# Layer 0 of a graph-attention stack: accumulators of half a PSUM bank, fed row by row, and a fourth bank for search products

## The chip, the cores and the metric

The kernel runs on one core of a Trainium2 chip. The metric is the device time of one execution in microseconds (us), as the median of three runs. A separate profiled execution gives the trace that is read here.

## The reference

Four graph-attention layers follow each other on 3327 nodes with 256 features; after each layer the input is added and the rows are normalised. The change is in layer 0 alone:

```python
g_src = nodes @ W_src_w.T + W_src_b
g_tgt = nodes @ W_tgt_w.T + W_tgt_b
g = leaky_relu(g_src[:, None, :] + g_tgt[None, :, :], 0.2)
score = einsum('ijc,c->ij', g, a_w)
score = where(adj_mat != 0, score, -inf)
weights = softmax(score, axis=1)
x = layernorm(nodes + weights @ g_tgt)
```

The adjacency matrix is random with about 1% ones, so a node has some 32 neighbours and at most 56. Layers 1 to 3 work on the same adjacency matrix densely.

## The kernel before

Layer 0 is the function `sparse0`. It works only on existing edges. The nodes form 26 tiles of 128 rows, in four sets of 4, 7, 9 and 6 tiles (`SETS`). Two kinds of work run side by side.

**The search** (`neighbours`, from L523) finds, for each row, the column numbers of its ones. A row of 3327 columns is cut into seven banks (six of 512 columns and one of 255). `convert` (L535, ScalarE) turns a loaded piece of the adjacency matrix to bf16. `fill` (L548, TensorE) makes, per bank, a product in PSUM that holds the column number where there is a one (the buffers `v`). `scan` (L572, VectorE) takes the eight largest of each of five stretches of that bank (L579). After seven banks `sort` and `note` (L581, L594) make the list of the tile. The loop at L644 walks over the banks: at position g it issues the product of bank g+2 and then the scan of bank g. The buffers of tag `v` are three PSUM banks used in turn, and `pss` (L482, the projection of a tile's source rows), `key_row` (L622), `sorted` (L702) and `early` (L1129) take their turn among them. When a set is searched, its rows are put in order of their number of neighbours, so that a tile needs only as many gathers as its longest row (`LEVELS`, `SEATS`).

**The attention** walks through the gather parts (`parts`, L308), each up to four neighbours of one tile. GpSimd fetches one neighbour's row for each of the 128 nodes with one indirect DMA (L912, into buffers `g`), and VectorE scores it (L932 and L938, against `a_ps`, a PSUM bank in which small products of `excess` also lie: L781, L803, L823). When a tile is scored, `weights` makes the softmax weights, and `combine` (L997) adds up the weighted rows: ScalarE scales each row in place (L1012), TensorE adds it to a PSUM accumulator by a product with the identity (L1015). The accumulator `acc` is a full bank of two halves of 256 columns, and two neighbours at a time (512 columns) are added, one into each half. `add_input` (L1035) then scales and adds both halves (L1041 and L1045), and the sum is written out by GpSimd. There are two such accumulator banks; `pt` (L467, the projection of a tile's target rows) uses the same two.

The eight PSUM banks are: accumulators 2, `v` 3, `a_ps` 1, `minus` 2 (the source row of a tile, negated, L925).

The order on every engine is written out by hand: a loop over the parts (L1282) takes some steps of the search (spread so that a set's lists are there in time, `owed`), then the actions that are due at this part (`due`: `combine` in the eight parts after a tile's last one, `add_input` at the tenth, L1237 to L1239), then the gather of the part eight places ahead, then the scoring. The first set is searched ahead of that, together with the projection of all target rows (`targets`, L461), which fill the table that is gathered from (L1178 to L1201). The last tile adds only its first four parts on TensorE and the rest on VectorE (`add_aside`, L982). Layer 1 follows at once (L1723, products with the dense attention weights), and its TensorE work is queued behind that of layer 0.

Of the kernel before, what the change touches and what calls it, by code (L numbers as in the profile page):

```python
# [19 lines left out]
P = 128  # L20
# [30 lines left out]
def gat_stack(  # L51
# [226 lines left out]
    def sparse0(lost):  # L278
        GROUP, TURNS, LEAD, SPREAD = 4, 22, 8, 8
        starts = [sum(SETS[:s]) for s in range(len(SETS))]  # L280
        with ExitStack() as s0:
# [179 lines left out]
            def targets(it):  # L461

                xt, pn = columns_of(it)
                row = io0.tile([P, ROW], F32, tag="row", name="row", bufs=3)
                if pn < P:
                    nc.vector.memset(row, 0.0)
                pt = ps0.tile([P, BANK], F32, tag="acc", name="pt")  # L467
                project(pt, xt, pn, w_tgt)
                yield
                nc.scalar.copy(row[:pn], pt[:pn, :ROW])  # L470
                nc.gpsimd.dma_start(table_d[1 + it * P : 1 + it * P + pn, :], row[:pn])
                if it < SETS[0]:
                    nc.gpsimd.dma_start(own_rows(it)[:, AT_TGT:], row)
                elif pn < P:
                    nc.gpsimd.dma_start(own_rows(it)[pn:, AT_TGT:], row[pn:])
                yield

            def sources(it):

                xt, pn = columns_of(it)  # L480
                yield
                pss = ps0.tile([P, BANK], F32, tag="v", name="pss", bufs=3)  # L482
                project(pss, xt, pn, w_src, bs_row)
                yield
                minus = find.tile([P, dim + 1], F32, tag="minus", name="minus")
                if pn < P:
                    nc.vector.memset(minus, 0.0)
                    nc.scalar.dma_start(own_rows(it)[pn:, AT_X : AT_X + dim], minus[pn:, :dim])
                nc.scalar.mul(minus[:pn], pss[:pn, : dim + 1], -1.0)  # L489
                nc.scalar.dma_start(own_rows(it)[:, : dim + 1], minus)  # L490
                yield
# [26 lines left out]
            listed = {}  # L518

            def steps_of(s):  # L520
                return SETS[s] * (len(banks_n) + 2) + 8

            def neighbours(s):  # L523

# [23 lines left out]
                def fill(t, b):  # L548
                    lo, hi = banks_n[b]
                    w, at0 = hi - lo, lo % PIECE  # L550
                    adj_b = cast[t, lo // PIECE]
                    v = filled[t, b] = ps0.tile([P, BANK], F32, tag="v", name="v", bufs=3)
                    nc.tensor.matmul(v[:, :w], leads[:, b, :], code[:, :w], start=True, stop=False)  # L553
                    own0 = (starts[s] + t) * P
                    own = lo <= own0 < hi
                    nc.tensor.matmul(  # L556
                        v[:, :w], raised, adj_b[:, at0 : at0 + w], start=False, stop=not own
                    )
                    if own:
                        wo = min(P, hi - own0)  # L560
                        nc.tensor.matmul(
                            v[:, own0 - lo : own0 - lo + wo], raised, minus_one[:, :wo],
                            start=False, stop=True,
                        )
                        flag = find.tile([P, P], BF16, tag="flag", name="flag", bufs=1)
                        nc.vector.scalar_tensor_tensor(
                            flag[:, :wo], adj_b[:, own0 % PIECE : own0 % PIECE + wo], 1.0,
                            ident[:, :wo], op0=ALU.mult, op1=ALU.mult,
                            accum_out=marks[:, starts[s] + t, 1:2],
                        )  # L570
# [48 lines left out]
                    return key_diag  # L619

                def spread_key(t, key_diag):
                    row = ps0.tile([P, BANK], F32, tag="v", name="key_row", bufs=3)  # L622
                    nc.tensor.matmul(row[:, :P], ones, key_diag, start=True, stop=True)
                    return row

# [15 lines left out]
                for k in all_pieces[:3] if s else ():  # L641
                    load(s, *k)
                convert(*all_pieces[0])
                for g in range(-2, len(units)):  # L644
                    if g >= 0:
                        t, b = units[g]
                        if b in (1, 2, 3):
                            turn_key(t - 1, b - 1)
                        if b == 0:
                            of_rows[t] = sources(starts[s] + t)  # L650
                        if b in (0, 4, 5):
                            next(of_rows[t])
                    if g + 2 < len(units):
                        t, b = units[g + 2]
                        if b % 2 == 0:
                            at = all_pieces.index((t, b // 2))
                            if at + 1 < len(all_pieces):
                                convert(*all_pieces[at + 1])
                            if at + 3 < len(all_pieces):
                                load(s, *all_pieces[at + 3])  # L660
                        fill(t, b)
                    if g >= 0:
                        t, b = units[g]
                        scan(t, b)
                        if b == len(banks_n) - 1:
                            yield
                            sort(t)
                            yield
                            note(t)
                    yield  # L670
# [17 lines left out]
            def permute(size, ranks, ranks_i, payloads):  # L688
# [10 lines left out]
                )  # L699
                cols = size * (KMAX + 2)  # L700
                assert cols <= BANK and n >= P
                sorted_ps = ps0.tile([P, BANK], F32, tag="v", name="sorted", bufs=3)  # L702
                for t in range(size):
                    unit = io0.tile([P, P], F32, tag="key_diag", name="unit")
                    nc.vector.tensor_scalar(
# [178 lines left out]
            def combine_excess(s):  # L884
                over = extras[s]
                rows = over["g"][:, 0, :dim]
                nc.scalar.activation(rows, rows, AF.Copy, scale=over["weight"][:, 1:2])
                nc.tensor.matmul(
                    held[s, 0]["acc"][:, 0, :], over["back"], rows, start=False, stop=False
                )  # L890

            def gather_own(s, t):
# [85 lines left out]
                )  # L978

            ASIDE = 4  # L980

            def add_aside(entry, k0, k1, first):  # L982

# [13 lines left out]
            def combine(s, t, i):  # L997

                entry = held[s, t]
                kt, w = places[s, t], entry["w"]  # L1000
                cuts = cuts_of(seats[s, t])
                k0, k1 = cuts[i]
                final = seats[s, t]
                if (s, t) == tiles[-1]:
                    final = cuts[ASIDE - 1][1]
                    if i >= ASIDE:
                        add_aside(entry, k0, k1, first=i == ASIDE)
                        return
                g = entry["g"][k0]

                def scale(rows, k):
                    nc.scalar.activation(rows, rows, AF.Copy, scale=w[:, k : k + 1])  # L1012

                def add_up(dst, rows, start=False, stop=False):
                    nc.tensor.matmul(dst, ident, rows, start=start, stop=stop)  # L1015

                if i == 0:
                    entry["acc"] = ps0.tile([P, 2, dim], F32, tag="acc", name="acc0")
                    own_row = entry["own"][:, AT_TGT : AT_TGT + dim]
                    scale(own_row, kt)  # L1020
                for k in range(k0, k1):
                    scale(g[:, k - k0, :dim], k)
                acc, m = entry["acc"], k1 - k0
                pairs = [g[:, k : k + 2, :dim] for k in range(0, m - 1, 2)]
                if i == 0:
                    for x, rows in enumerate(pairs):
                        add_up(acc, rows, start=x == 0)
                    add_up(acc[:, 0, :], own_row)
                else:
                    if m % 2:  # L1030
                        add_up(acc[:, 1, :], g[:, m - 1, :dim])
                    for x, rows in enumerate(pairs):
                        add_up(acc, rows, stop=k1 == final and x == len(pairs) - 1)

            def add_input(s, t):  # L1035

# [2 lines left out]
                nc.vector.reciprocal(inv, entry["total"])  # L1039
                y = entry["y"] = io0.tile([P, dim], F32, tag="hs", name="hs")  # L1040
                nc.vector.scalar_tensor_tensor(  # L1041
                    y, entry["acc"][:, 0, :], inv, entry["own"][:, AT_X : AT_X + dim],
                    op0=ALU.mult, op1=ALU.add,
                )
                nc.vector.scalar_tensor_tensor(  # L1045
                    y, entry["acc"][:, 1, :], inv, y, op0=ALU.mult, op1=ALU.add
                )
                nc.vector.tensor_add(y, y, bt_rows)
                if "aside" in entry:
# [76 lines left out]
                    rows1.append(t)  # L1126

            def early_bank():
                return ps0.tile([P, BANK], F32, tag="v", name="early", bufs=3)  # L1129

            def dots_next(x):
                for c in range(kc):
# [43 lines left out]


            first = neighbours(0)  # L1178
            next(first)
            next(first)  # L1180
            score_columns()
# [982 lines left out]
```

## Time and profile before

| | us |
|---|---|
| median of three runs | 3398.66 (3390.78 to 3407.27) |
| the profiled execution | 2952.55 |
| its span | 2950.7 |
| GpSimd: gathers (L912), 894 of them | 851.6 busy, first start 88.6, last start 1342.6 |
| first layer-1 product on TensorE (L1723) | 1367.12 |

The profiled execution is 446 us shorter than the median of the runs; the profile shows only itself. Layer 0 takes the span's first 1367 us, layers 1 to 3 the rest. In the page's slices, a digit is a busy share in tenths. In the timeline, a line is the start, the duration, the engine, the line of the kernel, what is written from what, and in brackets how long the engine had been idle and what ended that. In the list of waits, a line is who waited for whom, the total, how many times, and the longest.

### The profile page before, as it was taken

The page shows a single profiled execution, that of the slowest core. Times are in us where ns is not written, and L with a number is a line of the kernel's source. Part 1 is how long each engine was busy: PE and PEld are TensorE (multiplying, and loading weights), DVE is VectorE, ACT ScalarE, POOL GpSimd, SP SyncE. Part 2 cuts the span into 40 slices and gives each one's busy share as a digit, 9 for nine tenths or more (in the row PEclk, how much of TensorE's full clock was granted, in tenths as well). Part 3 has the DMA queues.
Part 4 walks back from the last instruction along what each step waited for, and adds up shares of the span by engine and source line. Part 5 has one row for each costly group of instructions (what it writes and reads, how often), then busy time and mean ns, then how long its engine had stood idle before and what let it go on. Part 6 is the DMA issues. An engine that isn't in the chain of part 4 may idle for free.

```text
span 2950.7 us, 45073 instructions
## 1 busy us (share of the span) xinstructions
PE 2317.0 (79%) x15862; PEld 1359.2 (46%) x15862; DVE 2134.7 (72%) x5615; ACT 852.4 (29%) x2381; POOL 992.3 (34%) x1061
## 2 busy tenths in 40 slices
PE   7466667556545416657899999999999999999997
PEld 4222323222222103325688888763546567534332
DVE  6789789968776518755455521138999999999997
ACT  3244445434334304533344411110010110111211
POOL 2676767777777777772000000000000000000000
PEclk8576777777767757889999999999999999999998
DMA  7685655545644435545776733331222222212211
GB/s 234 194 263 147 187 166 171 141 130 158 166 112 114 112 107 124 171 120 165 227 208 195 201 82 107 110 98 45 73 61 84 75 80 63 73 43 62 59 47 48
DMA packets 183854, 370.50 MB, mean 126 GB/s; under 512 B 35772, under 2 KB 124707, under 8 KB 182596
## 3 DMA queue, kind: packets, MB, share of 16 engines
q1 hardware_dynamic: 103994, 178.49, 21.4%
q0 software_dynamic: 51008, 155.70, 19.1%
q10 hardware_dynamic: 28618, 33.33, 3.3%
q8 instruction: 128, 2.10, 0.3%
q14 instruction: 106, 0.87, 0.1%
HBM read 327.52 MB, written 46.23 MB: 127 GB/s over the span
## 4 chain that ended last, share of the span: by engine, by line
PE 46%; DVE 4%; DMA 2%; issue 0%; ACT 0%; SPq 0%; DVEq 0%; POOL 0%; POOLq 0%; ACTq 0%
PE acc L1773 18%; PE acc L1723 16%; PE acc L1781 9%; DVE e L1629 3%; PE misc L1557 3%; DMA at<-at_d 1%; PE misc L1666 0%; DMA at_d<-at 0%; DMA at_i<-in_adj_t_dram 0%; DVE stats L1952 0%; DVE h L1950 0%; DVE h L1745 0%; DVE both L1947 0%; PE misc L1822 0%; DMA dst<-in_l_att_dram 0%
## 5 line engine op out<-in xcount | busy, mean ns | idle before, releaser
L912 POOL DMA_INDIRECT g<-table_d,lst x894 | 851.6, 953 | 273.1 <-issue 245.6
L1629 DVE SCALAR_TENSOR_TENSOR e<-rate,feat,at 128x896 f32<-128x896 f32 (+4 forms) x832 | 843.6, 1080 | 59.2 <-PE acc L1781 47.7
L1015 PE MATMUL acc<-g,ident 128*128 128x512 f32 (+1 forms) x896 | 505.5, 708 | 262.3 <-ACT g L1012 246.1
L1773 PE MATMUL acc<-e,feat 128*32 128x384 f32 (+2 forms) x6656 | 692.7, 515 | 6.7 <-DVE h L1745 4.2
L1773 PEld LDWEIGHTS acc<-e,feat 128*32 128x32 f32 x6656 | 307.1, 110 | 300.2 <-issue 161.5
L1015 PEld LDWEIGHTS acc<-g,ident 128*128 128x128 f32 x896 | 195.1, 228 | 481.6 <-ACT g L1012 364.6
L1781 PE MATMUL acc<-e,feat 128*32 128x384 f32 (+3 forms) x3328 | 383.3, 512 | 0.0
L1012 ACT ACTIVATE g<-g,w 128x256 f32<-128x256 f32 x883 | 365.4, 495 | 0.4 <-ACT minus L489 0.4
L932 DVE TENSOR_TENSOR y<-g,minus_ps 128x1028 f32<-128x1028 f32 (+2 forms) x233 | 273.4, 1173 | 125.0 <-DMA g<-table_d,lst 115.9
L938 DVE SCALAR_TENSOR_TENSOR y<-y,a_ps 128x257 f32<-128x257 f32 x894 | 324.3, 418 | 24.8 <-PE a_ps L781 6.2
L1723 PE MATMUL acc<-feat,e 128*128 128x257 f32 (+2 forms) x1352 | 303.5, 382 | 9.1 <-DVE inv L1744 6.4
L1723 PEld LDWEIGHTS acc<-feat,e 128*128 128x128 f32 (+2 forms) x1352 | 254.9, 191 | 46.9 <-issue 9.3
L1723 PE MATMUL acc<-feat,at 128*128 128x257 bf16 (+2 forms) x2028 | 237.9, 274 | 4.2 <-DMA at<-at_d 4.0
L1781 PEld LDWEIGHTS acc<-e,feat 128*32 128x32 f32 (+1 forms) x3328 | 162.0, 110 | 130.8 <-issue 88.1
L1723 PEld LDWEIGHTS <-at 128*128 128x128 bf16 (+2 forms) x2028 | 198.8, 99 | 38.0 <-DMA at<-at_d 4.5
L553 PE MATMUL v<-code,leads 65*128 65x512 bf16 (+1 forms) x182 | 83.1, 458 | 156.9 <-DVE cand L579 111.0
L1629 DVE SCALAR_TENSOR_TENSOR e<-rate,feat,at_i 128x896 f32<-128x896 f32 (+2 forms) x104 | 112.3, 1081 | 92.1 <-DMA at_i<-in_adj_t_dram 44.6
L579 DVE MAX8 cand<-v 128x8 f32<-128x104 f32 (+2 forms) x858 | 158.9, 260 | 21.7 <-PE v L556 21.7
L1609 POOL DMA_DIRECT2D rate3b_d<-rate_rows x4 | 2.1, 520 | 449.8 <-ACT rate_rows L1608 449.8
L251 POOL TENSOR_TENSOR rstds<-rstds,minus_half 128x7 f32<-128x7 f32 (+1 forms) x8 | 12.0, 1506 | 385.0 <-DVE rstds L250 385.0
L1959 POOL TENSOR_TENSOR rstds<-rstds,minus_half 128x7 f32<-128x7 f32 (+1 forms) x4 | 7.6, 1912 | 384.5 <-DVE rstds L1958 384.5
L1656 ACT CAST at<-at_i 128x896 bf16<-128x896 int32 (+2 forms) x104 | 92.1, 885 | 111.9 <-DMA at_i<-in_adj_t_dram 75.5
(253 smaller groups left out, 1864.6 us busy)
## 6 DMA issues: line engine op xcount, KB each, us to landing
adj_i<-in_adj_dram SPq DMA_DIRECT2D x75, 512.0 KB
at<-at_d SPq DMA_DIRECT2D x150, 224.0 KB
at_i<-in_adj_t_dram SPq DMA_DIRECT2D x50, 448.0 KB
at<-at_d SPq DMA_DIRECT2D x75, 192.0 KB
at<-at_d SPq DMA_DIRECT2D x75, 191.8 KB
g<-table_d,lst POOLq DMA_INDIRECT x894, 2.8
at_d<-at ACTq DMA_DIRECT2D x50, 224.0 KB
at_i<-in_adj_t_dram SPq DMA_DIRECT2D x25, 384.0 KB
```

Source lines behind the costliest of these rows:

```text
L579: nc.vector.max(spread[:, c0 + c, :], view(v[:, :w]))
L912: nc.gpsimd.indirect_dma_start(out=g[:, k - k0, :], out_offset=None, in_=table_d[:, :], in_offset=bass.IndirectOffsetOnAxis(ap=entry["lst" ...
L932: nc.vector.tensor_tensor(y, rows, minus_src[:, None, :].to_broadcast([P, m, dim + 1]), op=ALU.max)
L938: nc.vector.scalar_tensor_tensor(y, y, 1.0, a_ps[:, : dim + 1], op0=ALU.mult, op1=ALU.mult, accum_out=sc)
L1012: nc.scalar.activation(rows, rows, AF.Copy, scale=w[:, k : k + 1])
L1015: nc.tensor.matmul(dst, ident, rows, start=start, stop=stop)
L1557: nc.tensor.matmul(pacc[:pn, : dim + self.extra], ht[:, k, :pn], self.weight[:, k, :], start=(k == 0), stop=(k == kc - 1),)
L1629: nc.vector.scalar_tensor_tensor(e[:pn, : c1 - c0], self.rate[b][:pn, h_of, : c1 - c0], q, at[:pn, : c1 - c0], op0=ALU.max, op1=ALU.mult,)
L1656: nc.scalar.copy(at[:pn, :w], at_i[:pn, :w])
L1723: nc.tensor.matmul(accs[s][:pn, : dim + 1], a[:pj, s * P : s * P + pn], f[:pj, : dim + 1], start=(j == 0 and part == 0), stop=(j == nt - 1 ...
L1773: nc.tensor.matmul(accs[x][p][q : q + 32, : hi - lo], f[:pj, at0 : at0 + 32], es[at0 // hd][:pj, lo:hi], start=(j == 0), stop=(j == nt - 1),)
L1781: nc.tensor.matmul(accs[x][pairs][h_of * 32 : (h_of + 1) * 32, : hi - lo], f[:pj, dim + h_of : dim + h_of + 1].to_broadcast([pj, 32]), es[ ...
```

## The change

It has two parts, both in layer 0.

An accumulator is now half a bank. One bank (`both`, tag `acc`, one buffer) is allocated once, and the tiles use its two halves in turn. `combine` adds each scaled row by itself, 256 columns wide, the tile's own row first. `add_input` has one operation less, since there is one sum instead of two.

The bank that this frees goes to the tag `v`, which now has four. The search issues the product of bank g+3, instead of g+2, ahead of the scan of bank g; the loop has one step more at its beginning, which the plan (`steps_of`) and the first calls take into account. The projection `pt` moves from the two banks of tag `acc` to the two of tag `minus`.

```diff
-                pt = ps0.tile([P, BANK], F32, tag="acc", name="pt")
+                pt = ps0.tile([P, BANK], F32, tag="minus", name="pt")
...
-                pss = ps0.tile([P, BANK], F32, tag="v", name="pss", bufs=3)
+                pss = ps0.tile([P, BANK], F32, tag="v", name="pss", bufs=4)
...
-                return SETS[s] * (len(banks_n) + 2) + 8
+                return SETS[s] * (len(banks_n) + 2) + 9
...
-                    v = filled[t, b] = ps0.tile([P, BANK], F32, tag="v", name="v", bufs=3)
+                    v = filled[t, b] = ps0.tile([P, BANK], F32, tag="v", name="v", bufs=4)
...
-                for g in range(-2, len(units)):
+                for g in range(-3, len(units)):
...
-                    if g + 2 < len(units):
-                        t, b = units[g + 2]
+                    if g + 3 < len(units):
+                        t, b = units[g + 3]
...
-                    held[s, 0]["acc"][:, 0, :], over["back"], rows, start=False, stop=False
+                    held[s, 0]["acc"], over["back"], rows, start=False, stop=False
...
+            both = ps0.tile([P, 2, dim], F32, tag="acc", name="acc0", bufs=1)
+            halves = [both[:, 0, :], both[:, 1, :]]
...
                 if i == 0:
-                    entry["acc"] = ps0.tile([P, 2, dim], F32, tag="acc", name="acc0")
+                    entry["acc"] = halves.pop(0)
+                    halves.append(entry["acc"])
                     own_row = entry["own"][:, AT_TGT : AT_TGT + dim]
                     scale(own_row, kt)
                 for k in range(k0, k1):
                     scale(g[:, k - k0, :dim], k)
-                acc, m = entry["acc"], k1 - k0
-                pairs = [g[:, k : k + 2, :dim] for k in range(0, m - 1, 2)]
+                acc = entry["acc"]
                 if i == 0:
-                    for x, rows in enumerate(pairs):
-                        add_up(acc, rows, start=x == 0)
-                    add_up(acc[:, 0, :], own_row)
-                else:
-                    if m % 2:
-                        add_up(acc[:, 1, :], g[:, m - 1, :dim])
-                    for x, rows in enumerate(pairs):
-                        add_up(acc, rows, stop=k1 == final and x == len(pairs) - 1)
+                    add_up(acc, own_row, start=True)
+                for k in range(k0, k1):
+                    add_up(acc, g[:, k - k0, :dim], stop=k == final - 1)
...
                 nc.vector.scalar_tensor_tensor(
-                    y, entry["acc"][:, 0, :], inv, entry["own"][:, AT_X : AT_X + dim],
+                    y, entry["acc"], inv, entry["own"][:, AT_X : AT_X + dim],
                     op0=ALU.mult, op1=ALU.add,
                 )
-                nc.vector.scalar_tensor_tensor(
-                    y, entry["acc"][:, 1, :], inv, y, op0=ALU.mult, op1=ALU.add
-                )
...
             first = neighbours(0)
+            next(first)
             next(first)
             next(first)
```

The remaining lines of the diff give `key_row`, `sorted` and `early` the same four buffers as `v`.

More of the change, by code (lines that the diff above doesn't have):

```diff
@@ L621, in spread_key @@
                 def spread_key(t, key_diag):
-                    row = ps0.tile([P, BANK], F32, tag="v", name="key_row", bufs=3)
+                    row = ps0.tile([P, BANK], F32, tag="v", name="key_row", bufs=4)
                     nc.tensor.matmul(row[:, :P], ones, key_diag, start=True, stop=True)
@@ L701, in permute @@
                 assert cols <= BANK and n >= P
-                sorted_ps = ps0.tile([P, BANK], F32, tag="v", name="sorted", bufs=3)
+                sorted_ps = ps0.tile([P, BANK], F32, tag="v", name="sorted", bufs=4)
                 for t in range(size):
@@ L1128, in early_bank @@
             def early_bank():
-                return ps0.tile([P, BANK], F32, tag="v", name="early", bufs=3)
+                return ps0.tile([P, BANK], F32, tag="v", name="early", bufs=4)
             def dots_next(x):
```

## The prediction

> **What bounds the kernel now.** I read the page's slices first, then a table of busy times by stage, then GpSimd's timeline for its idle gaps, then the waits of VectorE in the stages where those gaps lie, and last the timelines of VectorE and TensorE for one searched tile. The page:
>
> ```profile
> PE   7466667556545416657899999999999999999997
> POOL 2676767777777777772000000000000000000000
> PEclk8576777777767757889999999999999999999998
> L912 POOL DMA_INDIRECT g<-table_d,lst x894 | 851.6, 953 | 273.1 <-issue 245.6
> L938 DVE SCALAR_TENSOR_TENSOR y<-y,a_ps 128x257 f32<-128x257 f32 x894 | 324.3, 418 | 24.8 <-PE a_ps L781 6.2
> ```
>
> TensorE is nearly full from slice 19 on, but the change is in the slices before, and there TensorE is half busy at a reduced clock. GpSimd's level 7 is in fact a full engine: a gather takes 953 ns, and some 0.30 us follow in which nothing is waited for, so one gather costs 1.257 us. From the first gather (88.6 us) to the last (1342.6) GpSimd hardly rests. These are all its gaps over 1 us in that time (two views of its timeline, and the first lines show what begins and ends it):
>
> ```profile
> 87.21 1.06 POOL L897 DMA_INDIRECT own_of<-own_d,lst  x1 [8.88 <-DVE flag L566]
> 226.59 0.95 POOL L897 DMA_INDIRECT own_of<-own_d,lst  x1 [3.50 <-DVE y_over L845]
> 246.34 0.95 POOL L912 DMA_INDIRECT g<-table_d,lst  x1 [1.13 <-PE acc L1015]
> 262.73 1.00 POOL L731 DMA_INDIRECT lists_d<-payload,ranks_i  x1 [9.15 <-DVE ranks_i L682]
> 404.38 0.95 POOL L897 DMA_INDIRECT own_of<-own_d,lst  x1 [10.86 <-DVE hs L1041]
> 1342.57 0.95 POOL L912 DMA_INDIRECT g<-table_d,lst  x1 [0.30 <-issue]
> ```
>
> The middle four gaps are 24.6 us. So layer 0 has three stretches with different limits: a head of 87 us until the first lists are there; 87 to 404 us, where GpSimd runs into VectorE four times; and from 404 us on GpSimd alone. After 404 nothing that TensorE or VectorE saves can be worth anything until the tail. VectorE's waits, the first line for 0 to 87 us, the others for 87 to 404:
>
> ```profile
> DVE cand L579 <- PE v L556: 13.6, 9, 2.5
> ...
> DVE seat L800 <- PE a_ps L803: 14.4, 7, 6.0
> DVE cand L579 <- PE v L556: 6.9, 6, 1.9
> DVE y L938 <- PE a_ps L781: 4.6, 1, 4.6
> 87.00:404.00 317.00, 191.60 (x495) 87.36 (x493) 267.34 (x1208) 121.24 (x316) 222.81 (x233) 0.69 0.67 194
> ```
>
> The last line is the table of stages: in these 317 us TensorE is busy 191.6, VectorE 267.3, at a granted clock of 0.69. VectorE is late by its own work and by waits for products in `v` (L579) and for small products in `a_ps` that stand behind others on TensorE.
>
> **What the Trainium skill says.** "PSUM — Partial Sum Buffer", section "PSUM bank collisions raise a hardware error", asks that engines be kept apart by bank and quadrant, not by address. So two halves of one bank don't make two independent accumulators. The order of the changed kernel's waits agrees: `add_input` of one half waits for the newest product into either half, and the next product waits for `add_input`. The trace of before has a bank per tile and can't show it. "TensorE: Matmul & The Clock Gate", section "Part 1: The HAM clock gate", says that an idle TensorE runs at half clock until it has been busy for a while. The trace agrees: successive 128x512 bf16 products start 0.43 us apart at 33.71 and 0.22 us apart at 27.21. The same page, section "Back-to-back issue gap", gives a further 2.5 ns per product (its isolated gap, warm). The trace is dearer: four fp32 records of 512 columns take 1.88 us (at 337.90), four of 260 take 1.04 us (at 24.88), so 512 columns in two pieces cost about 0.05 us more than in one.
>
> **The change, part by part.**
>
> *Search ahead, in the head.* The second tile of the first set, VectorE first, then two releases on TensorE:
>
> ```profile
> 26.19 3.52 DVE L579 MAX8 cand<-v 128x8 f32<-128x104 f32 x20
> 32.22 0.96 DVE L579 MAX8 cand<-v 128x8 f32<-128x104 f32 x5 [2.51 <-PE v L556]
> 35.41 0.29 DVE L566 SCALAR_TENSOR_TENSOR flag<-adj_b,ident 128x128 bf16<-128x128 bf16 x1 [2.23 <-ACT adj_b L543]
> 38.52 0.57 DVE L579 MAX8 cand<-v 128x8 f32<-128x85 f32 x3 [1.93 <-PE v L556]
> ...
> 27.21 0.39 PE L553 MATMUL v<-code,leads 65*128 65x512 bf16 x1 [1.29 <-DVE cand L579]
> 30.02 0.80 PE L623 MATMUL key_row<-key_diag,ones 128*128 128x128 f32 x2 [2.21 <-ACT key_diag L618]
> ```
>
> Four banks are scanned, then the fifth, the flag and the seventh are each waited for: 6.7 us in this tile, 2.9, 5.9 and 3.7 in the others. With one product more in hand, the fifth is there when TensorE stands at `key_row` until 30.8; the sixth comes at the fifth's place (ready about 32.2), the last one at about 34.4 instead of 38.5. That is 4 us at the tile's end. But TensorE still has the same projections to do, so by the fourth bank of the next tile I leave 2.5. I take 2.5 us for the second and third tile, 1.5 for the fourth, 0.5 for the first: 7 us. Bounds: 0 (the projections, whose rows also wait on DMAs, set the pace) and 12. The conversion on ScalarE and the loads on SP move one step earlier with it; nothing on those queues is short there. `pt` keeps two buffers, and those of tag `minus` are free until the first `lay_out`: nothing.
>
> *Search ahead, 87 to 404.* The five waits of 0.4 to 1.9 us for a tile's last bank (6.6 of the 6.9 us) have `pss` ahead of them on TensorE; three ahead, `pss` stands before the next tile's first bank, which is needed only after some 4 us of sorting. All 6.6 go. The 23.9 us for `a_ps` (L803 14.4, L781 4.6, others 4.9) stay in kind, but TensorE need no longer stand at `key_row` or `pss` until a scan frees a buffer (2.3 us before 347.9 by the profile; 2.8 before 357.7, whose cause it doesn't name, just ahead of the two longest): I take 4, bounds -3 and 10.
>
> *One addition less on VectorE.* L1045 with its gap is 0.52 us; three lie before the gap at 404: 1.6. The others are covered by VectorE's own waits for gathers.
>
> *Row by row on TensorE.* 883 rows and 26 own rows make 1818 records instead of 948. At 0.05 us a row that is 44 us, about twice that at half clock; by the page's 2.5 ns it would be 2, with every additional weight load (228 ns) exposed 198. I take 60. It is hidden by TensorE's idle time (588 us of layer 0's 1367) and by ScalarE, for whose scaled rows TensorE waits anyway; a row can now start while the next one is scaled. Until 404 it is 141 rows. Without that cover it would count in full.
>
> *The new waits.* Ten of the 25 `add_input` that have a successor wait for the next tile's first five to nine rows. Behind them on VectorE stand a scoring and the scans. The rows need the softmax, 0.5 us, five scalings of 0.45, and five products of about 1 us that overlap them: 4 to 8 us, of which at least one part's scoring and search (5 us) has passed. So 0 to 3 us each; only one lies before 404 (the third), and VectorE has there waited for a later product anyway. I take nothing, since later VectorE idles for gathers. At the tail it shows: `add_input` of the last tile but one stood at 1353.5 and now waits for products that ended at 1359.5; the 5.5 us of `add_aside` behind it end at 1366.4 instead of 1360.5, just past the last sum (1366.0), while one addition (0.5) falls away. I take 0.5 us loss, bounds -0.5 and +6.
>
> Sum: 7 + 6.6 + 4 + 1.6 - 0.5 = 18.7 us; the middle terms (12.2) fit into the 24.6 us of gaps. Layers 1 to 3 keep their instructions and start earlier by it. 2952.55 - 18.7 = 2933.9 us for the profiled execution. The median of the runs lies 446.1 above, and the trace doesn't show where; I carry the difference over unchanged: 3380.0.
>
> **Rivals.**
>
> *The runs are slower on TensorE.* If the 446 us come from a lower clock, the waits for TensorE (13.6, 6.9 and 23.9 us) are longer in the runs, and so is what is removed: at one and a half times, about 30 us, 3369. For it: most of the span is TensorE's. Against: nothing shows the clock of the runs.
>
> *Only the head moves.* TensorE's order after 87 us still puts small products behind four rows at a time, and the freed waits come back as `a_ps` waits. Then some 6 us are left: 3393.
>
> *TensorE becomes the slower partner.* In 87 to 404 us the pace is VectorE's 267 us of work. 141 rows with exposed weight loads add 32 us to TensorE's 192; at the half clock (0.69 to 0.50) that makes 192 x 1.38 + 32 x 1.38 = 309. It decides from the point where TensorE passes 267 us, a clock of 0.58. Then GpSimd gaps grow by 309 - 267 = 42 us, less some 12 from the head and the scans: +30, 3429. For it: TensorE's digits there are 6 and the clock is already low. Against: more work on TensorE raises the clock rather than lowers it, and most rows wait for ScalarE.
>
> **How the numbers follow.** Forecast 50% (3373 to 3389, two thirds of it past 0.5%), lower clock 18% (3359 to 3373), head only 18% (3387 to 3401), TensorE 14%. About 0.5%, 17 us, is what a measurement of this kernel can tell from no change: faster 34 + 18 = 52%, within 16 + 18 = 34%, slower 14%. The range 3358 to 3402 holds the first three cases and leaves the last out; all lower bounds of the sum together give 0.8 us more than before (3399), all upper ones 30.7 less (3368), so they lie in it.
>
> **What would show it.** Right: the first gather starts near 81 us; the L579 waits for `v` are almost gone; the gaps of GpSimd before 404 fall from 24.6 to about 12 us; L1015's successor has 1818 records; the first L1723 product is near 1348. Wrong: an unchanged first gather (the projections set the head), new gaps of GpSimd after 404 that end on `add_input` (the shared bank), or TensorE busy over 267 us where it was 192.

## The result and the profile after

| | before, us | changed, us | ratio (95% interval) |
|---|---|---|---|
| first comparison, medians of 6 runs each | 3402.46 | 3363.82 | 0.9905 (0.9880 to 0.9931) |
| repeated in a later set of runs | 3399.05 | 3362.56 | 0.9898 (0.9875 to 0.9921) |
| repeated in another set | 2951.80 | 2940.12 | 0.9962 (0.9950 to 0.9975) |

Runs that were measured together (one set, "a call" in the quoted expectations) all fell into one of two conditions, in which before takes either some 2950 us or some 3400 us in every run, so the profile that the prediction was made from, with its 2952.55 us, shows the 2950 condition, and the runs that it had to forecast were in the 3400 condition.

The change is a gain in both: 32 to 35 us in the 3400 condition by the ratios (36 to 39 by the medians), 11 us in the 2950 condition. The forecast was 18.7.

The changed kernel's first profile shows the 3400 condition. Its page, the same lines as were shown of before:

```profile
PE   7156365453345433444458999999999999999997
POOL 2734644655545666645730000000000000000000
PEclk8557667676666766666779999999999999999998
L912 POOL DMA_INDIRECT g<-table_d,lst x894 | 851.6, 953 | 417.8 <-issue 259.3
L938 DVE SCALAR_TENSOR_TENSOR y<-y,a_ps 128x257 f32<-128x257 f32 x894 | 324.6, 418 | 280.6 <-remote 228.0
```

The gathers take the same 953 ns, but GpSimd's digits, a steady 7 in before's first profile, are now 3 to 7, and its idle time ahead of gathers is 417.8 us instead of 273.1. L938 on VectorE takes as long as ever and waits 280.6 us instead of 24.8 ("remote" is a wait whose end the profile lays to no instruction). To see what is the change's and what is the condition's, the like has to be set beside the like. Before in the 3400 condition (`before_third`):

```profile
PE   6145355544245433444548999999999999999997
POOL 2734644655635656656630000000000000000000
PEclk8557666676666667656779999999999999999998
```

It looks the same. And the changed kernel in the 2950 condition (`after_again`):

```profile
PE   7466667555554417657899999999999999999997
POOL 2676777777777777771000000000000000000000
PEclk9577678767777657879999999999999999999998
```

That is the steady 7 again. So what catches the eye between before's first profile and the changed kernel's is the condition, not the change. The difference lies in layer 0: layer 1's first product starts at 1358.83 us in a trace of before in the 2950 condition (`before_again`) and at 1817.89 in the 3400 one, and layers 1 to 3 then take 1586 and 1589 us.

Of the change itself, the traces of the 2950 condition show this. GpSimd's gaps over 1 us between the first gather and 412 us, from its timeline, before (`before_again`), then changed (`after_again`):

```profile
141.19 0.95 POOL L912 DMA_INDIRECT g<-table_d,lst  x1 [1.83 <-DMA own_of<-own_d,lst]
220.75 0.95 POOL L897 DMA_INDIRECT own_of<-own_d,lst  x1 [1.48 <-DVE y_over L845]
240.50 0.95 POOL L912 DMA_INDIRECT g<-table_d,lst  x1 [1.12 <-PE acc L1015]
256.89 1.00 POOL L731 DMA_INDIRECT lists_d<-payload,ranks_i  x1 [9.15 <-DVE ranks_i L682]
...
398.45 0.95 POOL L897 DMA_INDIRECT own_of<-own_d,lst  x1 [10.54 <-DVE hs L1041]
```

```profile
183.26 0.96 POOL L912 DMA_INDIRECT g<-table_d,lst  x1 [1.16 <-issue]
254.87 1.00 POOL L731 DMA_INDIRECT lists_d<-payload,ranks_i  x1 [8.80 <-DVE ranks_i L682]
270.99 0.99 POOL L731 DMA_INDIRECT lists_d<-payload,ranks_i  x1 [1.07 <-DMA lists_d<-payload,ranks_i]
...
390.75 1.02 POOL L897 DMA_INDIRECT own_of<-own_d,lst  x1 [4.00 <-DVE hs L1038]
```

24.1 us have become 15.0 (the forecast had 12). The two long ones ended on VectorE before and still do; the one near 255 us is nearly as long as it was, the one near 390 is shorter by 6.5. Not all of the 9.1 us last: from the first gather to the last it is 1252.7 us before and 1248.8 us changed, 3.9 less, for GpSimd has a new gap of 2.1 us at 595.6, and its own work in that stretch took 937.0 instead of 933.9 us. These two profiled executions took 2946.76 and 2941.77 us, so the pair of traces holds 5.0 of the 11 us that the runs give. VectorE's waits, changed kernel, 82 to 400 us:

```profile
DVE seat L800 <- PE a_ps L803: 16.1, 8, 3.7
DVE y L938 <- PE a_ps L803: 5.2, 2, 3.4
DVE y_own L938 <- PE a_ps L803: 4.3, 1, 4.3
DVE y L938 <- PE a_ps L781: 2.0, 1, 2.0
```

The waits for `v` (L579), 7.2 us in `before_again`, are gone from the list. The waits for `a_ps` are 27.6 us; in `before_again` they were 23.9 (14.3, 4.7, 3.0 and 1.9). The forecast had these fall by 4.

### The profile page after: what moved, and what is told of

Read it like the earlier page. It is cut to its first block, busy times and chain, and to the rows that moved or that the text cites. A ratio compares the mean times of both kernels' runs of the same rounds, so it can differ in the third digit from the quotient of the medians.

```text
span 3367.8 us, 47149 instructions
## 1 busy us (share of the span) xinstructions
PE 2374.6 (71%) x16703; PEld 1584.2 (47%) x16732; DVE 2134.7 (63%) x5589; ACT 855.2 (25%) x2381; POOL 993.0 (29%) x1061
## 4 chain that ended last, share of the span: by engine, by line
PE 47%; DVE 16%; issue 13%; another core or an unknown queue 11%; POOL 6%; DMA 4%; ACT 3%; ACTq 0%; DVEq 0%; SPq 0%; POOLq 0%
PE acc L1768 16%; PE acc L1718 13%; PE acc L1776 8%; PE acc L1017 5%; POOL g L912 5%; DVE y L938 4%; DVE y L932 3%; PE misc L1552 2%; DVE e L1624 2%; DVE cand L579 2%; ACT g L1014 1%; DVE found L587 1%; DVE cand L589 1%; DMA at_d<-at 1%
## 5 line engine op out<-in xcount | busy, mean ns | idle before, releaser
L912 POOL DMA_INDIRECT g<-table_d,lst x894 | 851.6, 953 | 417.8 <-issue 259.3
L1017 PE MATMUL acc<-g,ident 128*128 128x256 f32 x1766 | 542.0, 468 | 211.6 <-ACT g L1014 86.1
L1017 PEld LDWEIGHTS acc<-g,ident 128*128 128x128 f32 x1766 | 418.2, 242 | 321.3 <-issue 101.3
L938 DVE SCALAR_TENSOR_TENSOR y<-y,a_ps 128x257 f32<-128x257 f32 x894 | 324.6, 418 | 280.6 <-remote 228.0
L932 DVE TENSOR_TENSOR y<-g,minus_ps 128x1028 f32<-128x1028 f32 (+2 forms) x233 | 273.0, 1172 | 24.8 <-issue 20.3
L579 DVE MAX8 cand<-v 128x8 f32<-128x104 f32 (+2 forms) x858 | 168.2, 261 | 98.4 <-issue 90.8
L1017 PE MATMUL acc<-own_of,ident 128*128 128x256 f32 x52 | 28.6, 651 | 197.9 <-ACT own_of L1014 63.1
L553 PEld LDWEIGHTS <-leads 65*128 65x128 bf16 x182 | 22.8, 125 | 264.2 <-remote 134.2
L251 POOL TENSOR_TENSOR rstds<-rstds,minus_half 128x7 f32<-128x7 f32 (+1 forms) x8 | 12.1, 1507 | 385.4 <-DVE rstds L250 385.4
```

Source lines behind the costliest of these rows:

```text
L579: nc.vector.max(spread[:, c0 + c, :], view(v[:, :w]))
L912: nc.gpsimd.indirect_dma_start(out=g[:, k - k0, :], out_offset=None, in_=table_d[:, :], in_offset=bass.IndirectOffsetOnAxis(ap=entry["lst" ...
L932: nc.vector.tensor_tensor(y, rows, minus_src[:, None, :].to_broadcast([P, m, dim + 1]), op=ALU.max)
L938: nc.vector.scalar_tensor_tensor(y, y, 1.0, a_ps[:, : dim + 1], op0=ALU.mult, op1=ALU.mult, accum_out=sc)
```

## The experiments

**Before, profiled again** (no edit).

> The kernel before, profiled once more. Its first profile had a span of 2950.7 us while its runs took 3390 to 3411; the changed kernel's profile (3367.8 us) is like its runs. Theory S (crawl): in the runs, once GpSimd has issued gathers for about 10 us without a pause, VectorE, TensorE and ScalarE crawl until GpSimd pauses (in the changed kernel's trace VectorE is busy 0.80 of the first 10 us of such a stretch and 0.25 from 15 us on). It expects about 3400 us, layer 0 ending near 1815 us, the same fall of VectorE's busy share inside long stretches, and layers 1 to 3 unchanged at about 1584 us. Rival C (clock): the missing 446 us are a lower TensorE clock spread over the whole kernel; then layers 1 to 3 are longer too, and VectorE's and ScalarE's instructions follow each other as in the first profile. If this profile is again near 2951 us, the comparison stays open.

It came to the 2950 condition: 2948.04 us beside 2950.33. So the cause of the 446 us stayed open here. The first gather started at 83.1 us, against 88.6 in the first trace of the same kernel: a single trace's head is known to some 5 us only.

**Single rows alone.** The changed kernel with the search of before:

```diff
-for g in range(-3, len(units)):
+for g in range(-2, len(units)):
...
-v = filled[t, b] = ps0.tile([P, BANK], F32, tag="v", name="v", bufs=4)
+v = filled[t, b] = ps0.tile([P, BANK], F32, tag="v", name="v", bufs=3)
```

(with `g + 2`, the plan and the other users of tag `v` set back as well.)

> The change without its search part: row by row into half a bank, but three buffers v and two products ahead as before (the freed bank is unused). My prediction puts the whole gain into the search and its buffers, with 1.6 us for the missing addition on VectorE: it expects 3401 against 3402 for before, within 0.5%. Theory S: VectorE's and TensorE's work in layer 0 isn't covered by gathers as priced, so 25 additions less (13 us) shorten the kernel and some 60 us more of TensorE work lengthen it; it expects a change of -15 to +20 us. A rival in which the single rows are the gain (a row starts before the next one is scaled) expects about -25 us, that is most of the -32 to -38 measured.

2946.93 us, ratio 0.9994 (0.9985 to 1.0003), in the 2950 condition: no difference, as the prediction had it. Twice as many records, the weight loads that go with them, one shared bank and one addition less together come to nothing.

**Four buffers, two products ahead.** The changed kernel with only the order of the search set back:

```diff
-for g in range(-3, len(units)):
+for g in range(-2, len(units)):
...
-if g + 3 < len(units):
-    t, b = units[g + 3]
+if g + 2 < len(units):
+    t, b = units[g + 2]
```

> The changed kernel with four buffers v, but search products only two ahead as before. My prediction puts the gain into the third product in hand: it expects about 3398, some 4 us under before for the additional buffer alone. If the fourth buffer alone is the gain (key_row and the projections no longer hold a scan's buffer), about 3375. If the row-by-row half is the gain, near the changed kernel's 3364.

2930.61 us, ratio 0.9933 (0.9920 to 0.9946): 19.7 us less than before, in the set in which single rows alone gave nothing. The two kernels differ only in the fourth buffer, so in this condition that buffer is a gain by itself. The expectation of 4 us for the buffer was wrong by a factor of five. (The times expected were written for the 3400 condition; the differences count.) GpSimd's gaps over 1 us up to 412 us are down to two:

```profile
145.25 0.95 POOL L912 DMA_INDIRECT g<-table_d,lst  x1 [1.24 <-DMA own_of<-own_d,lst]
254.82 1.00 POOL L731 DMA_INDIRECT lists_d<-payload,ranks_i  x1 [5.48 <-DVE ranks_i L682]
```

The gap of 10.5 us near 400 is gone.

**A pause on GpSimd before each gather.**

```diff
 for k in range(k0, k1):
+    nc.gpsimd.memset(g[:, k - k0, :128], 0.0)
     nc.gpsimd.indirect_dma_start(
```

> The changed kernel with a memset of 128 columns of the gather's own row on GpSimd ahead of every gather: nothing else is changed. If nothing but GpSimd's own time counted, 894 times at least 0.2 us are added to layer 0: 180 us more, some 3545. Theory S: what makes the others crawl is an unbroken stream of gathers, and a pause in each keeps them at their normal pace; then layer 0 is bounded by 894 x (1.26 + 0.3 to 0.5) = 1395 to 1575 us after the first 82, so it ends at 1480 to 1660 instead of 1785, and the kernel takes 3060 to 3240 us. If the crawl doesn't depend on pauses, 3545 or more.

3107.56 us, in the 2950 condition, where there was no crawl to cure; so it doesn't test theory S. It does show that in this condition layer 0 is GpSimd's: GpSimd is busy 198 us longer than in the changed kernel (1193.2 and 995.2 us), and against that kernel's 2940.12 (of another set) the time is 167 us more, 0.19 us for each of 894 gathers.

**The changed kernel again** (no edit).

> The changed kernel once more, on a chip where before takes what its profile took (2950 in the last call) if this call finds one. My forecast for that is -18.7 us: 2932. With two products ahead and the fourth buffer it was 2930.6. Theory B (the buffer is the gain): the third product in hand adds nothing, -18 to -21 us. Theory L (looking ahead is worth its own part, in the head): the first gather 3 to 7 us earlier, -23 to -27 us. If this call finds a chip on which before takes 3400, -30 to -40 as in the first comparison.

2940.12 us against 2951.80: 11.2 us by the ratio. Neither theory's number: the kernel with one product fewer in hand is better by 8.5 us, and the two ratios' intervals (0.9950 to 0.9975, and 0.9920 to 0.9946) don't meet. In the 2950 condition, and across two sets, the third product costs something (or the one step more per set in its plan, which wasn't separated from it).

**The freed bank to `key_row` alone, and to `pss` alone** (both from single rows alone):

```diff
-row = ps0.tile([P, BANK], F32, tag="v", name="key_row", bufs=3)
+row = ps0.tile([P, BANK], F32, tag="k", name="key_row", bufs=1)
```

(and the same edit to `pss` in the other kernel.)

> Single rows into half a bank, two products ahead, three buffers v, and the freed bank given to key_row alone (the product between a tile's sort and its key row). With the bank unused the kernel is like before (2946.9 against 2950.3); with the bank as a fourth v it is 19.7 us faster. Theory K (key_row standing in the v sequence holds TensorE up until a scan is done, and the small products for VectorE stand behind it): most of the 19.7 us, 2930 to 2936, and VectorE's waits for a_ps in 84 to 400 us fall from 24 to about 10. Theory P (the projections pss are what holds it): 2944 to 2950.

> The same with the freed bank given to pss alone (the projection of a tile's source rows). Theory P: 2930 to 2936, and VectorE's waits for v (L579) in 84 to 400 us fall from 7 to under 2. Theory K: 2942 to 2948, since only the waits for a tile's last bank (6 us, partly hidden) go. If both this and the other give about half, the buffers are simply too few and any one more does it.

2937.63 and 2940.91 us, ratios 0.9957 (0.9945 to 0.9969) and 0.9962 (0.9949 to 0.9975). Each gives a little over half of the 19.7 us, and both are level with the changed kernel: neither small product is by itself the one that blocks, and the reading that was put down for this case is that any one buffer more does it. What sets the kernel with 19.7 us apart from these is seen in TensorE's waits from 84 to 400 us. Each fence is one kernel: before (`before_again`), the changed one (`after_again`), four buffers and two ahead (`look2`):

```profile
PE v L553 <- DVE cand L579: 42.9, 11, 10.1
...
PE key_row L623 <- DVE cand L579: 13.6, 6, 3.0
```

```profile
PE v L553 <- DVE cand L579: 51.2, 14, 11.8
...
PE key_row L623 <- DVE cand L579: 5.9, 3, 3.0
```

```profile
PE v L553 <- DVE cand L579: 19.0, 7, 10.8
```

TensorE stands until a scan has freed a buffer for 56.5 us before, 57.1 in the changed kernel and 19.0 with two ahead in four. The small products for VectorE stand behind in TensorE's order, as one place in the changed kernel shows (`after_again`):

```profile
126.34 2.05 PE L452 MATMUL pss<-w_src,xt 128*128 128x257 f32 x4 [2.92 <-issue]
...
131.16 0.31 PE L561 MATMUL v<-minus_one,raised 128*128 128x128 bf16 x1
131.26 0.96 PE L803 MATMUL a_ps<-given,seat 128*128 128x4 f32 x4
131.84 0.29 DVE L800 TENSOR_SCALAR seat<-upto,there 128x128 f32<-128x128 f32 x1 [3.27 <-PE a_ps L803]
```

VectorE is done with the seats at 128.57, but TensorE, which has stood for 2.92 us until 126.34, first makes the projection and two banks' products. VectorE's waits with two ahead in four, 82 to 400 us:

```profile
DVE seat L800 <- PE a_ps L803: 10.0, 7, 3.3
...
DVE cand L579 <- PE v L556: 1.9, 3, 1.2
```

So with one spare buffer 13.9 of the 23.9 us of waits for `a_ps` are gone, and the third product in hand uses that buffer up: in four buffers the product of bank g+3 needs the buffer of bank g-1, as that of bank g+2 does in three. With `key_row` or `pss` moved away TensorE still waits 55.2 and 60.0 us for scans (the latter 46.4 and 13.6 at `key_row`), and VectorE 22.7 and 19.2 us for `a_ps`. These waits therefore tell the gain of 19.7 us from gains of 11 to 13, but not those from none: single rows alone waited 67.0 us for scans and gained nothing. What gives the first 11 to 13 us isn't shown.

**Four buffers and two ahead, the changed kernel, and one ahead in three, in one set.** The edit of the last is `range(-1, ...)` and `g + 1` with three buffers `v`.

> Four buffers v and two products ahead, now in one call with the changed kernel (three ahead), since the two were measured in different calls: -19.7 us and -11.7 us against before. Theory W (a buffer that is not yet needed is worth more than a product that is): TensorE takes its work in order, and with three ahead in four buffers it stands at v until the scan of the bank before has ended, as with two ahead in three; its waits for scans in 84 to 400 us were 56.5 us before, 57.1 in the changed kernel and 19.0 here. So this kernel is again 6 to 10 us faster than the changed one. Rival N (the difference came from the two calls): within 3 us of it.

> The changed kernel beside it. Theory W: 9 to 13 us under before, that is 6 to 10 us above the kernel with two ahead. Rival N: the same time as that one. On a chip where before takes 3400, 30 to 40 us under before; then the trace of before in this call shows where.

> Single rows into half a bank, three buffers v (the freed bank unused), one product ahead instead of two. Theory W: one buffer is spare as with two ahead in four, so TensorE's waits for scans in 84 to 400 us fall from 67 (two ahead in three) to about 20, and VectorE's waits for a_ps from 25 to about 10 us, while its waits for v rise from 8.5 to 15 or 25; the two nearly cancel: 2938 to 2950. Rival L (looking ahead is what counts): slower than before by 10 us or more, with waits for v far over 25 us and those for a_ps as before.

> The kernel before, for its trace beside the others of this call. Where before takes 2950: gaps of GpSimd of 24 us between 84 and 412 us, as in its two earlier traces, and a first gather between 83 and 89 us (its spread tells what of the head a single trace can show). Where it takes 3400: VectorE busy 0.8 in the first 10 us of a stretch of gathers without a pause and under 0.3 from 15 us on, as in the first trace of the changed kernel.

This was the 3400 condition. Against before's 3399.05: 3358.89 (0.9876, 0.9843 to 0.9908), 3362.56 (0.9898, 0.9875 to 0.9921) and 3383.97 (0.9945, 0.9926 to 0.9964). The first two aren't told apart here. One ahead in three gains 19 us by the ratio, where rival L had it lose 10 or more; but its trace can't judge theory W: what fills TensorE's and VectorE's waits from 84 to 400 us in this condition is something else, in before as well. For `before_third` VectorE waited only 5.5 us for `a_ps` at L800.

That something is what theory S was about, and `before_third` shows it. I took all stretches in which indirect DMAs follow each other on GpSimd within 0.4 us, and from the start of each VectorE's busy share (worked out from the traces `before_third`, `after_third`, `before_again` and `after_again`, in this order):

| since the stretch began, us | before, 3400 | changed, 3400 | before, 2950 | changed, 2950 |
|---|---|---|---|---|
| 0 to 10 | 0.79, 0.85 | 0.82, 0.79 | 0.83, 0.88 | 0.76, 0.81 |
| 10 to 15 | 0.59 | 0.45 | 0.88 | 0.91 |
| 15 to 20 | 0.32 | 0.28 | 0.86 | 0.83 |
| 20 to 25 | 0.18 | 0.20 | 0.72 | 0.69 |
| 25 to 30 | 0.23 | 0.08 | 0.76 | 0.79 |

(0 to 10 us in two halves. TensorE and ScalarE fall alike: from 0.56 and 0.40 to 0.25 and 0.15 at 20 to 25 us, before, 3400 condition.) A piece of such a crawl, VectorE in the changed kernel's first trace:

```profile
177.74 0.27 DVE L579 MAX8 cand<-v 128x8 f32<-128x96 f32 x1 [0.42 <-issue]
178.44 0.28 DVE L579 MAX8 cand<-v 128x8 f32<-128x104 f32 x1 [0.43 <-issue]
179.14 0.28 DVE L579 MAX8 cand<-v 128x8 f32<-128x104 f32 x1 [0.42 <-issue]
```

The bank scanned is there, no wait for another engine is recorded, and one instruction starts every 0.70 us; right after, five of them run in 0.96 us.

**Four more operations on VectorE per tile** (the changed kernel):

```diff
 nc.vector.tensor_add(y, y, bt_rows)
+for _ in range(4):
+    nc.vector.scalar_tensor_tensor(y, y, 1.0, y, op0=ALU.mult, op1=ALU.max)
```

> The changed kernel with four more operations of 128x256 on VectorE in every add_input (y, multiplied by one, and the larger of that and y: y stays what it is): 104 operations of about 0.43 us, 45 us of VectorE work in layer 0; with three tiles before 404 us and the last one exposed it prices the work that the change takes from VectorE (one operation a tile). On a chip where before takes 2950: theory H of the prediction, VectorE's work after 404 us is covered by gathers: 4 x 0.43 x 4 = 7 us slower than the changed kernel, that is some 4 us under before; if it is not covered, 30 to 45 us slower. On a chip where before takes 3400: theory S (there GpSimd waits for VectorE some 400 us in layer 0, so VectorE's work counts): 35 to 90 us slower than the changed kernel, level with before or above it; if it is covered there too, 5 to 10 us slower.

The 2950 condition: 2942.14 against 2950.44, ratio 0.9975 (0.9966 to 0.9983). By the ratios it is 3.8 us slower than the changed kernel, and the two intervals overlap (0.9950 to 0.9975): theory H. Of some 45 us more of VectorE's work nearly all is covered. What the same would cost in the 3400 condition isn't known.

## Why the prediction was right, and where its sizes were off

The direction was right, and in the 2950 condition the place too: the gain comes from the search and its buffers, and single rows cost nothing. That the range held is luck. 3363.82 us lies in it, but not in the forecast's own part (3373 to 3389): it lies where the rival of a lower clock was put, whose cause the traces don't show. The gain, 32 us by the ratio and 39 by the medians, is more than all upper bounds of the sum together (30.7). The terms, in the condition that the profile showed (2950):

| step | predicted gain, us | shown |
|---|---|---|
| head | 7 | not resolved: first gather 82.7 to 88.6 in five traces with two ahead in three buffers (mean 84.4), 82.1 to 85.0 in three with three ahead (83.7) |
| waits for `v`, 87 to 404 us | 6.6 | gone, as said |
| waits for `a_ps` | 4 (-3 to 10) | -3.7: from 23.9 to 27.6 us |
| one addition less | 1.6 | not resolved: 104 more cost 3.8, with intervals that overlap |
| rows, hidden, and the shared bank | 0 | 0: ratio 0.9994, with the 1818 records forecast; the sums wait 20.8 us for rows with single rows alone, 20.5 in `before_again` |
| tail | -0.5 (-6 to 0.5) | 1 to 2.5: from the last gather to the first layer-1 product 24.5 and 23.1 us before, 22.0 changed |
| sum | 18.7 | 11.2 (7.4 to 14.8, by the ratio) |

The middle terms are waits of VectorE in one trace, and not all of them reach GpSimd, so the column doesn't add up to its last line. The signs that were set down are mixed too: the first gather, forecast near 81 us, starts at 84.1 in `after_again` and at 83.1 in `before_again`, and the first product of layer 1, forecast near 1348, at 1354.91. Two pieces instead of one were read as 0.05 us dearer; by the figures given there it is 0.10 for a pair (1.04 against 0.94), that is the 0.05 a row that the sum then uses.

The step that failed is "TensorE need no longer stand at `key_row` or `pss` until a scan frees a buffer: I take 4". For four buffers and two products ahead the waits did fall, and by more (13.9). With three ahead the new buffer is taken at once by a product that VectorE doesn't want yet, TensorE stands for a scan as long as before (57.1 us against 56.5), and the waits for `a_ps` rose by 3.7.

In the head the wait moved. Before (`before_again`), then changed (`after_again`), VectorE, 0 to 84 us:

```profile
DVE cand L579 <- PE v L556: 9.3, 10, 1.7
DVE flag L566 <- ACT adj_b L543: 5.2, 4, 2.2
```

```profile
DVE flag L566 <- ACT adj_b L543: 11.0, 4, 5.1
DVE cand L579 <- PE v L556: 2.7, 2, 1.5
```

`flag` is issued with the product of its bank, so it too is one bank earlier, and VectorE waits there for ScalarE's conversion instead: of the 6.6 us that the waits for `v` lost, 5.8 came back. I had looked at the conversion's queue and not at who waits for it; `flag` was in the lines that I showed. With two ahead in four buffers the two waits are 12.8 and 6.0 us and the first gather starts at 87.7 (`look2`), so in the head it is the third product, if anything, that helps, and not the fourth buffer.

The cost of single rows on TensorE was put at 60 us, hidden; TensorE's busy time is 2320.7 us with single rows alone and 2322.1 in `before_again`. The 60 us weren't there to be hidden: TensorE's busy time in these rows is 528.9 us (`after_again`) against 534.4. (A record took 716 ns in the mean, nearly all of them of pairs, and one of a single row takes 442; a product is two records, and they overlap.)

The last step, "I carry the difference over unchanged", decided what the forecast missed. In the 3400 condition layer 0 is another regime: GpSimd no longer sets the pace alone, it waits for engines that crawl while it works. In `before_third` these are the longest of GpSimd's waits for another engine from 84 to 1800 us:

```profile
POOL sums_d L1057 <- DVE hs L1048: 105.5, 12, 23.8
POOL own_of L836 <- DVE taken_i L812: 61.5, 3, 46.9
POOL g L912 <- PE acc L1015: 60.9, 25, 9.8
```

There the terms of the sum don't apply. Layer 0 of before in three parts, beside two traces of the changed kernel in the same regime (first trace and `after_third`):

| us | before | changed |
|---|---|---|
| to the first gather | 88.1 | 83.7, 76.8 |
| first to last gather | 1667.3 | 1644.1, 1638.1 |
| last gather to the first layer-1 product | 62.5 | 55.2, 57.0 |

So 23 to 29 of the 35 to 46 us between these traces lie where the forecast allowed 12 for the middle, and not before 404 us alone: after 212 gathers, where the first trace of before has reached 404 us, the changed kernel is ahead by 14.4 and 10.3 us (counted from the first gather); the rest comes later. The first line of that list waits for the end of `add_input`, so the addition that it has lost (VectorE's busy time 2147.2 and 2134.7 us) is a candidate, and one product ahead in three buffers gains 19 us over before without the fourth bank. Which of the parts gives how much in this regime isn't settled: single rows alone and the added operations were both measured in the 2950 condition. The rival "the runs are slower on TensorE" had the size (30) and not the cause: the clock is lower (0.82 against 0.87), but all three engines crawl together, and only in layer 0; layers 1 to 3 take as long as ever (1589 and 1586 us).

The version with four buffers and two ahead is the best found: 19.7 us under before in the 2950 condition, 40 in the 3400 condition, where it isn't told apart from the changed kernel.

## What to carry to other kernels

A buffer that is added and a product that is issued one step earlier are two changes; on an engine that takes its work in order the second can spend what the first brings, as here in the 2950 condition, so try the buffer alone first. When work is moved ahead, follow every instruction that is issued with it to the engine that runs it, down to a small one like `flag`. And when a profile's own time is far from the runs, it may show another regime: terms from it hold for that regime only, and the difference shouldn't be carried over as a constant.

## What was not expected of the hardware

In some sets of runs, not in others, with the same kernel: from about 10 us of gathers without a pause on, VectorE, TensorE and ScalarE fall from 0.8, 0.6 and 0.4 busy to 0.2, 0.25 and 0.15 or less (`before_third`), in the piece shown with one VectorE instruction every 0.70 us and no wait for another engine recorded. Each gather takes 0.95 us in both conditions, and the packets of GpSimd's DMA queue take as long: 18.8% of 16 engines' 2945.0 us in `before_again`, 16.4% of 3407.3 us in `before_third`, that is 554 and 559 us an engine. Between these two traces it costs 459 us of layer 0. Before and changed kernel show it alike. What is short isn't shown, nor whether pauses between gathers avoid it, nor whether it belongs to the chip: three sets on three chips were in the 2950 condition, and the set with `before_third` was on a fourth.
